# Value matmuls on 64x64 tiles of the array and energy matmuls on 64x128 tiles, one key chunk at a time

## The chip, the cores and the metric

The kernel runs on one core of a Trainium2 chip. The metric is the device time of one execution in microseconds (us), the median of several. A profile of one execution is kept for every kernel; all views below are of such profiles.

## The reference, cut to what matters

```python
# x: (4, 64, 96, 96) float32; layer 0 works on its group norm g
q = einsum('bchw,oc->bohw', g, wq) + bq      # 8 channels; k alike; v has 64
energy = einsum('bcn,bcm->bnm', Q, K)        # 9216 x 9216 for each of 4 batches
att = sigmoid(energy)
out = einsum('bcm,bnm->bcn', V, att) + g
# ... a channel gate on out, the residual, then layer 1: a spectral
# convolution (a truncated FFT as small matmuls). The change is in layer 0 alone.
```

The 4 batches are taken as 2 pairs. In a pair the 9216 queries are 18 blocks of 512 and the 9216 keys 72 chunks of 128. So there are 2 x 18 x 72 = 2592 chunk visits, and each needs energies of two batches, one sigmoid over 128 x 1024, and values of two batches.

## The kernel before

P = 128, NB = 512, C = 64, NCH = 72. Energies are made from high and low parts of q and k so that the one-pass type (fp32r) keeps fp32 accuracy: 8 channels x 4 combinations of parts are 32 rows. Two chunks and two batches lie on four groups of 32 rows.

```python
# PSUM: ps_s 3 buffers of 2 banks, ps_a 2 buffers of 1 bank
def energies(n, jj, q):                        # two chunks of keys at once
    es = [ps_s.tile([P, 2, NB], F32, tag="s", ...) for i in range(2)]
    for i in range(2):
        for b in range(2):
            r = slice(32 * (2 * i + b), 32 * (2 * i + b) + 32)
            nc.tensor.matmul(es[i][:, b, :], kT[r, jj, :], q[r, :], start=True, stop=True)
    # ... one sigmoid per chunk: at <- es[i] (ScalarE)

def values(acc, jj, ats):                      # plain fp32
    for i in range(2):
        j = 2 * jj + i
        for b in range(2):
            half = slice(b * C, (b + 1) * C)
            nc.tensor.matmul(acc[half, :], vT[:, j, half], ats[i][:, b, :],
                             start=(j == 0), stop=(j == NCH - 1))

for n in range(NBLK):
    acc = ps_a.tile([P, NB], F32, tag="a", ...)
    for jj in range(NCH // 2):
        nxt = energies(n, jj + 1, q)           # (of the next block at the end)
        values(acc, jj, ats); ats = nxt
        # ... q of the next block is projected eight steps before the end
    # ... VectorE adds acc to xn, sums and maxima for the gate
```

## Time and profile before

| | before |
|---|---|
| time, median of 3 | 3697.69 us (3696.52 to 3698.01) |
| matrix engine (PE) busy | 96% of the span |
| ScalarE busy | 70% |
| the attention loop, both pairs | about 3030 of 3695 us |

A timeline row gives the start and length in us, the engine, the source line, the operation with what it writes and reads, the tile of the array in rows*columns, the shape, and the number of instructions merged into the row. PEld is a weight load. Brackets hold the idle time of the engine before the row and what ended it; "issue" means that the profile shows nothing it waited for. The record of a matmul begins when it goes to the array (after a change of tiling that is when its own weight load begins, 1001.87 and 1001.88 in the view of the changed kernel), and its end is modelled, so the distances between starts are what to trust. Below, a pass is one matmul record, a round is the passes that start together on different tiles, and a visit is the rounds of one kind of matmul, energies or values, before the other kind follows. The prediction below shows the page and one step of the loop.

### The profile page before, as it was taken

To read this page: it belongs to the slowest core of one execution; us is meant where nothing else is said; L and a number is where in the kernel's file an instruction comes from. 1 tells how busy PE (TensorE), PEld (TensorE's weight loads), DVE (VectorE), ACT (ScalarE), POOL (GpSimd) and SP (SyncE) were. 2 spreads that over 40 slices of the span, in tenths; PEclk is the share of its full clock that TensorE was granted. 3 is DMA by queue.
4 is the path that set the end of the run, shared out by engine and by line. 5 is a ranking of instruction groups with operands and counts; after the bars stand their busy time and mean duration, and the time that the engine had idled before them with its cause. 6 is when DMAs were issued, how large, how long until landed. Compare 5 with 4: busy or idle time off the path is not lost.

```text
span 3694.8 us, 44562 instructions
## 1 busy us (share of the span) xinstructions
PE 3564.6 (96%) x19088; PEld 1391.2 (38%) x19088; DVE 424.2 (11%) x810; ACT 2585.2 (70%) x2699; POOL 2.9 (0%) x10
## 2 busy tenths in 40 slices
PE   5999999999999999969999999999999999699999
PEld 3222222222222222232222222222222222289999
DVE  7000000000000000061000000000000000431033
ACT  1888888888888888826888888888888888511011
POOL 0000000000000000000000000000000000000000
PEclk8999999999999999989999999999999999855555
DMA  2000000000000000000000000000000000000311
GB/s 107 1 1 1 1 1 1 1 1 1 1 1 1 1 1 1 1 0 1 1 1 1 1 1 1 1 1 1 1 1 1 1 1 1 35 1 23 126 49 55
DMA packets 7222, 38.93 MB, mean 11 GB/s; under 512 B 1936, under 2 KB 2416, under 8 KB 3952
## 3 DMA queue, kind: packets, MB, share of 16 engines
q1 hardware_dynamic: 5184, 35.65, 2.6%
q8 instruction: 149, 2.44, 0.3%
q10 hardware_dynamic: 1840, 0.43, 0.1%
q14 instruction: 49, 0.40, 0.0%
HBM read 26.65 MB, written 9.44 MB: 10 GB/s over the span
## 4 chain that ended last, share of the span: by engine, by line
PE 94%; DVE 4%; DMA 0%; issue 0%; ACT 0%; ACTq 0%; POOL 0%; POOLq 0%; DVEq 0%
PE acc L225 66%; PE e L211 15%; PE pv L335 3%; PE pa L304 2%; PE py L371 2%; PE pz L362 2%; PE pq L199 1%; DVE stats L113 1%; PE pu L316 1%; PE pu L319 1%; DVE x L270 1%; DVE vT L188 1%; DVE strip L135 0%; DVE low_k L144 0%; PE pvt L349 0%; PE proj L184 0%
## 5 line engine op out<-in xcount | busy, mean ns | idle before, releaser
L216 ACT ACTIVATE at<-e 128x1024 f32<-128x1024 f32 x2592 | 2512.6, 1021 | 657.7 <-PE e L211 657.7
L225 PE MATMUL acc<-at,vT 128*64 128x512 f32 x10368 | 2513.9, 606 | 0.0
L225 PEld LDWEIGHTS acc<-at,vT 128*64 128x64 f32 x10368 | 629.5, 136 | 1062.3 <-issue 1061.2
L211 PE MATMUL e<-q,kT 32*128 32x512 f32 x5184 | 660.1, 498 | 12.7 <-DVE q L148 11.3
L211 PEld LDWEIGHTS e<-q,kT 32*128 32x128 f32 x5184 | 248.8, 182 | 1062.3 <-issue 1059.4
L143 DVE TENSOR_SCALAR full_q<-pq,bq 128x512 f32<-128x512 f32 x36 | 27.0, 750 | 2266.0 <-PE pq L199 2266.0
L335 PE MATMUL pv<-u,wt 128*64 128x12 f32 x1024 | 109.4, 261 | 0.0
L335 PEld LDWEIGHTS pv<-u,wt 128*64 128x64 f32 x1024 | 109.3, 227 | 0.2 <-issue 0.2
L245 DVE SCALAR_TENSOR_TENSOR xn<-acc,xn 128x512 f32<-128x512 f32 x36 | 24.9, 692 | 622.8 <-PE acc L225 622.8
L304 PE MATMUL pa<-fw_sb,xT 96*96 96x48 f32 x512 | 84.4, 361 | 1.3 <-ACT xT L110 1.3
L304 PEld LDWEIGHTS pa<-fw_sb,xT 96*96 96x96 f32 x512 | 84.1, 257 | 1.8 <-ACT xT L110 1.8
L371 PE MATMUL py<-gw_sb,z 32*128 32x96 f32 x384 | 82.5, 417 | 1.8 <-ACT z L110 1.8
L371 PEld LDWEIGHTS py<-gw_sb,z 32*128 32x128 f32 x384 | 82.1, 328 | 2.5 <-ACT z L110 2.5
L362 PE MATMUL pz<-gh_sb,vt 64*32 64x96 f32 x512 | 82.3, 363 | 0.0
L362 PEld LDWEIGHTS pz<-gh_sb,vt 64*32 64x32 f32 x512 | 81.6, 171 | 0.3 <-issue 0.3
L110 ACT COPY v<-pv 64x192 f32<-64x192 f32 x16 | 7.6, 477 | 101.4 <-PE pv L335 101.4
L110 ACT COPY z<-pz 32x384 f32<-32x384 f32 x32 | 25.4, 795 | 57.2 <-PE pz L362 57.2
L110 ACT COPY a<-pa 96x384 f32<-96x384 f32 x16 | 12.8, 800 | 73.4 <-PE pa L304 73.4
L128 PE MATMUL pv_l<-t_l,pav 128*128 128x1 f32 x8 | 2.3, 359 | 49.3 <-DVE t_l L126 49.3
L110 ACT COPY xT<-pt 96x512 f32<-96x512 f32 x24 | 14.0, 582 | 50.9 <-PE pt L296 50.9
L184 PE MATMUL proj<-wv,xn 128*128 128x128 f32 x288 | 49.4, 323 | 0.0
L178 PE MATMUL proj<-xn,wk 128*64 128x256 f32 x144 | 28.4, 477 | 20.8 <-DVE xn L135 20.4
(65 smaller groups left out, 757.1 us busy)
## 6 DMA issues: line engine op xcount, KB each, us to landing
wt<-in_spec_dram SPq DMA_DIRECT2D x16, 1024.0 KB, 4.9
x<-in_x_dram SPq DMA_DIRECT2D x8, 1152.0 KB, 7.8
out_dram<-x SPq DMA_DIRECT2D x12, 768.0 KB, 3.2
fh_sb<-in_fh_dram ACTq DMA_DIRECT2D x1, 72.0 KB
pav<-in_pairavg_dram ACTq DMA_DIRECT2D x1, 64.0 KB, 5.7
wk<-in_wk_dram ACTq DMA_DIRECT2D x1, 64.0 KB
wq<-in_wq_dram ACTq DMA_DIRECT2D x1, 64.0 KB, 4.3
bv<-in_bv_dram ACTq DMA_DIRECT2D x2, 32.0 KB, 3.6
```

What stands on the lines that cost most here:

```text
L110: nc.scalar.copy(dst, src)
L113: nc.vector.bn_stats(stats[:, s, :], xt[:, bass.ts(s, NB)])
L184: nc.tensor.matmul(pp[:, 1, bass.ts(i, P)], xn[:, bass.ts(j, P)], wv_sb, start=True, stop=True)
L188: nc.vector.tensor_tensor(vT[:, 4 * s:4 * s + 4, :], pp[:, 1, :].rearrange("p (i m) -> p i m", m=P), bv_sb.rearrange("p b c -> p (b c)").u ...
L199: nc.tensor.matmul(pq, wq_sb, xn[:, bass.ts(n, NB)], start=True, stop=True)
L211: nc.tensor.matmul(es[i][:, b, :], kT[r, jj, :], q[r, :], start=True, stop=True)
L216: nc.scalar.activation(at, es[i], AF.Sigmoid)
L225: nc.tensor.matmul(acc[half, :], vT[:, j, half], ats[i][:, b, :], start=(j == 0), stop=(j == NCH - 1))
L304: nc.tensor.matmul(pa[:H, bass.ts(i, 3 * KW)], xT[:, :, 8 * g + i], fw_sb, start=True, stop=True)
L335: nc.tensor.matmul(pv[:C, bass.ts(kw, 3 * B)], wt[:, i, kw, :], u[:, kh, kw, :, :].rearrange("q s b -> q (s b)"), start=True, stop=True)
L362: nc.tensor.matmul(pz[:2 * KW, bass.ts(i, H)], vt[:, b, :, :, o].rearrange("q e k -> q (e k)"), gh_sb, start=True, stop=True)
L371: nc.tensor.matmul(py[:, bass.ts(i, W)], z[:, 4 * g + i, :], gw_sb, start=True, stop=True)
```

## The change

Its intent is to have energies and values on tiles with the same number of rows. Values sum the two 64-key halves of a chunk in two banks, on four 64x64 tiles. Energies take one chunk of both batches, 64 rows each (of which q's zeros switch off the 32 of the other chunk).

```diff
-            tc.tile_pool(name="ps_s", bufs=3, space=PSUM) as ps_s, \
+            tc.tile_pool(name="ps_s", bufs=2, space=PSUM) as ps_s, \
...
-            def energies(n, jj, q):
-                es = [ps_s.tile([P, 2, NB], F32, tag="s", name=f"e_{p}_{n}_{jj}_{i}")
-                      for i in range(2)]
-                for i in range(2):
-                    for b in range(2):
-                        r = slice(32 * (2 * i + b), 32 * (2 * i + b) + 32)
-                        nc.tensor.matmul(es[i][:, b, :], kT[r, jj, :], q[r, :], ...)
+            def energies(n, j):
+                e = ps_s.tile([P, 2, NB], F32, tag="s", name=f"e_{p}_{n}_{j}")
+                for b in range(2):
+                    r = slice(64 * b, 64 * b + 64)
+                    nc.tensor.matmul(e[:, b, :], kT[r, j // 2, :], qs[n][j % 2][r, :], ...)
...
-                        nc.tensor.matmul(acc[half, :], vT[:, j, half], ats[i][:, b, :],
+                    for r in range(2):
+                        keys = slice(64 * r, 64 * r + 64)
+                        nc.tensor.matmul(acc[half, r, :], vT[keys, j, half], at[keys, b, :],
...
-                acc = ps_a.tile([P, NB], F32, tag="a", name=f"acc_{p}_{n}")
-                for jj in range(NCH // 2):
+                acc = ps_a.tile([P, 2, NB], F32, tag="a", name=f"acc_{p}_{n}")
+                for j in range(NCH):
...                     # energies of chunk j + 2, then values of chunk j
-                nc.vector.scalar_tensor_tensor(blk, acc, 1.0, blk, ALU.mult, ALU.add,
+                nc.vector.scalar_tensor_tensor(blk, acc[:, 0, :], 1.0, blk, ALU.mult, ALU.add)
+                nc.vector.scalar_tensor_tensor(blk, acc[:, 1, :], 1.0, blk, ALU.mult, ALU.add,
                                                accum_out=sums[:, n:n + 1])
...                     # q in two versions (even, odd chunks), k on rows in another order,
                      # projected on four 32-column tiles instead of two of 64 columns
```

More of the change, by code (lines that the diff above doesn't have):

```diff
@@ L72, in tile_kernel @@
     bk_sb = const.tile([P, 1], F32, tag="bk", name="bk")
-    split_sb = const.tile([P, 4], F32, tag="split", name="split_sb")
+    split_sb = const.tile([P, 6], F32, tag="split", name="split_sb")
     nc.scalar.dma_start(wk_sb, wk4)
@@ L135, in normalize, with split_parts @@
         nc.vector.tensor_scalar(dst, src, mr[:, 0:1], mr[:, 1:2], ALU.subtract, ALU.mult)
-    def split_parts(dst, src, bias, which, pool, name):
+    def split_parts(dsts, src, bias, first, pool, name):
         n = src.shape[-1]
@@ L141, in split_parts @@
         high = pool.tile([P, n], F32, tag="high", name=f"high_{name}")
-        low = pool.tile([P, n], F32, tag="low", name=f"low_{name}")
         nc.vector.tensor_scalar(full, src, bias, None, ALU.add)
-        nc.vector.tensor_scalar(low, src, bias, split_sb[:, 2 * which + 1:2 * which + 2],
-                                ALU.add, ALU.mult)
         nc.vector.tensor_scalar(high.bitcast(U32), full.bitcast(U32), HIGH, None,
                                 ALU.bitwise_and)
-        nc.vector.scalar_tensor_tensor(dst, high, split_sb[:, 2 * which:2 * which + 1], low,
-                                       ALU.mult, ALU.add)
+        for i, dst in enumerate(dsts):
+            f = 2 * (first + i)
+            low = pool.tile([P, n], F32, tag=f"low{i}", name=f"low{i}_{name}")
+            nc.vector.tensor_scalar(low, full, split_sb[:, f + 1:f + 2], None, ALU.mult)
+            nc.vector.scalar_tensor_tensor(dst, high, split_sb[:, f:f + 1], low,
+                                           ALU.mult, ALU.add)
     stats1 = []
@@ L156, in tile_kernel @@
             tc.tile_pool(name="q", bufs=2) as qp, \
+            tc.tile_pool(name="parts", bufs=1) as partp, \
             tc.tile_pool(name="att", bufs=4) as attp, \
-            tc.tile_pool(name="ps_s", bufs=3, space=PSUM) as ps_s, \
+            tc.tile_pool(name="ps_s", bufs=2, space=PSUM) as ps_s, \
             tc.tile_pool(name="ps_a", bufs=2, space=PSUM) as ps_a:
@@ L175, in tile_kernel @@
                 pp = ps_s.tile([P, 2, NB], F32, tag="s", name=f"proj_{p}_{s}")
-                for e in range(2):
-                    rows = slice(64 * e, 64 * e + 64)
+                for r in range(4):
+                    rows = slice(32 * r, 32 * r + 32)
                     nc.tensor.matmul(
                         pp[rows, 0, :2 * P].rearrange("p (a m) -> p a m", m=P), wk_sb[:, rows],
-                        xn[:, cols].rearrange("p (a e m) -> p a e m", e=2, m=P)[:, :, e, :],
+                        xn[:, cols].rearrange("p (a e m) -> p a e m", e=2, m=P)[:, :, r % 2, :],
                         start=True, stop=True)
@@ L185, in tile_kernel @@
                                      start=True, stop=True)
-                split_parts(kT[:, 2 * s:2 * s + 2, :].rearrange("p a m -> p (a m)"),
-                            pp[:, 0, :2 * P], bk_sb, 0, qp, f"k_{p}_{s}")
+                split_parts([kT[:, 2 * s:2 * s + 2, :].rearrange("p a m -> p (a m)")],
+                            pp[:, 0, :2 * P], bk_sb, 0, partp, f"k_{p}_{s}")
                 nc.vector.tensor_tensor(
@@ L199, in project_q @@
                 nc.tensor.matmul(pq, wq_sb, xn[:, bass.ts(n, NB)], start=True, stop=True)
-                q = qp.tile([P, NB], F32R, tag="q", name=f"q_{p}_{n}")
-                split_parts(q, pq, bq_sb, 1, qp, f"q_{p}_{n}")
-                return q
-            def energies(n, jj, q):
-                es = [ps_s.tile([P, 2, NB], F32, tag="s", name=f"e_{p}_{n}_{jj}_{i}")
-                      for i in range(2)]
-                for i in range(2):
-                    for b in range(2):
-                        r = slice(32 * (2 * i + b), 32 * (2 * i + b) + 32)
-                        nc.tensor.matmul(es[i][:, b, :], kT[r, jj, :], q[r, :],
-                                         start=True, stop=True)
-                ats = []
-                for i in range(2):
-                    at = attp.tile([P, 2, NB], F32, tag="att", name=f"at_{p}_{n}_{jj}_{i}")
-                    nc.scalar.activation(at, es[i], AF.Sigmoid)
-                    ats.append(at)
-                return ats
@@ L220, in values @@
-            def values(acc, jj, ats):
-                for i in range(2):
-                    j = 2 * jj + i
-                    for b in range(2):
+                q = [qp.tile([P, NB], F32R, tag=f"q{e}", name=f"q{e}_{p}_{n}")
+                     for e in range(2)]
+                split_parts(q, pq, bq_sb, 1, partp, f"q_{p}_{n}")
+                return q
+            def energies(n, j):
+                e = ps_s.tile([P, 2, NB], F32, tag="s", name=f"e_{p}_{n}_{j}")
+                for b in range(2):
+                    r = slice(64 * b, 64 * b + 64)
+                    nc.tensor.matmul(e[:, b, :], kT[r, j // 2, :], qs[n][j % 2][r, :],
+                                     start=True, stop=True)
+                at = attp.tile([P, 2, NB], F32, tag="att", name=f"at_{p}_{n}_{j}")
+                nc.scalar.activation(at, e, AF.Sigmoid)
+                return at
@@ L224, in values @@
+            def values(acc, j, at):
+                for b in range(2):
+                    for r in range(2):
                         half = slice(b * C, (b + 1) * C)
-                        nc.tensor.matmul(acc[half, :], vT[:, j, half], ats[i][:, b, :],
+                        keys = slice(64 * r, 64 * r + 64)
+                        nc.tensor.matmul(acc[half, r, :], vT[keys, j, half], at[keys, b, :],
                                          start=(j == 0), stop=(j == NCH - 1))
-            q = project_q(0)
@@ L229, in tile_kernel @@
-            ats = energies(0, 0, q)
+            steps = [(n, j) for n in range(NBLK) for j in range(NCH)]
+            qs = {0: project_q(0)}
+            ahead = [energies(*steps[0]), energies(*steps[1])]
             for n in range(NBLK):
-                acc = ps_a.tile([P, NB], F32, tag="a", name=f"acc_{p}_{n}")
-                for jj in range(NCH // 2):
-                    nxt = None
-                    if jj + 1 < NCH // 2:
-                        nxt = energies(n, jj + 1, q)
-                    elif n + 1 < NBLK:
-                        nxt = energies(n + 1, 0, q)
-                    values(acc, jj, ats)
-                    ats = nxt
-                    if jj == NCH // 2 - 8 and n + 1 < NBLK:
-                        qn = project_q(n + 1)
-                    if jj == NCH // 2 - 2 and n + 1 < NBLK:
-                        q = qn
+                acc = ps_a.tile([P, 2, NB], F32, tag="a", name=f"acc_{p}_{n}")
+                for j in range(NCH):
+                    if n * NCH + j + 2 < len(steps):
+                        ahead.append(energies(*steps[n * NCH + j + 2]))
+                    values(acc, j, ahead.pop(0))
+                    if j == NCH - 16 and n + 1 < NBLK:
+                        qs[n + 1] = project_q(n + 1)
@@ L414, in four @@
         for r in range(4):
-            o[r % 2, :, r] = w.T[:, None]
+            o[r // 2, :, r] = w.T[:, None]
         return o.reshape(P, P)
-    high = np.stack([np.tile(np.repeat(h, C8), 4) for h in ([1, 1, 0, 0], [1, 0, 1, 0])], 1)
+    kh, qh = [np.tile(np.repeat(h, C8), 4) for h in ([1, 1, 0, 0], [1, 0, 1, 0])]
+    even = np.arange(P) // 32 % 2 == 0
+    parts = np.stack([2 * kh - 1, 1 - kh] + [m * f for m in (even, ~even)
+                                             for f in (2 * qh - 1, 1 - qh)], 1)
     sent = {
@@ L423 @@
         "wk4": four(l0["wk"]), "bk4": np.tile(l0["bk"], 16).reshape(P, 1),
-        "split": np.stack([2 * high - 1, 1 - high], 2).reshape(P, 4).astype(np.float32),
+        "split": parts.astype(np.float32),
         "wvT": l0["wv"].T, "bv": l0["bv"].reshape(1, C),
```

## The prediction

> **What bounds the kernel now.** I read the page first: busy shares, then the chain that ended last, then the costliest groups.
>
> ```profile
> PE 3564.6 (96%) x19088; PEld 1391.2 (38%) x19088; DVE 424.2 (11%) x810; ACT 2585.2 (70%) x2699; POOL 2.9 (0%) x10
> ...
> PE acc L225 66%; PE e L211 15%; PE pv L335 3%; PE pa L304 2%; PE py L371 2%; PE pz L362 2%; PE pq L199 1%; DVE stats L113 1%; PE pu L316 1%; PE pu L319 1%; DVE x L270 1%; DVE vT L188 1%; DVE strip L135 0%; DVE low_k L144 0%; PE pvt L349 0%; PE proj L184 0%
> ...
> L216 ACT ACTIVATE at<-e 128x1024 f32<-128x1024 f32 x2592 | 2512.6, 1021 | 657.7 <-PE e L211 657.7
> L225 PE MATMUL acc<-at,vT 128*64 128x512 f32 x10368 | 2513.9, 606 | 0.0
> ...
> L211 PE MATMUL e<-q,kT 32*128 32x512 f32 x5184 | 660.1, 498 | 12.7 <-DVE q L148 11.3
> ```
>
> The reader sees that value matmuls (L225) and energy matmuls (L211) are 81% of the chain, that they never wait long (0.0 and 12.7 us idle), and that ScalarE, which waits 657.7 us for energies, is not the bound. "128*64" and "32*128" are the array tiles: rows by columns. The counts also tell the passes: there are 2 pairs x 18 blocks x 36 = 1296 steps of two key chunks, each with four value and four energy matmuls. So 10368 value records are two passes per plain fp32 matmul, and 5184 energy records are one pass per fp32r matmul.
>
> A busy matrix engine is not one at its peak, so next I read the timeline of one step in the middle (start us, length us, engine, line, operation, count):
>
> ```profile
> 1001.80 0.19 PEld L211 LDWEIGHTS e<-q,kT 32*128 32x128 f32 x4 [0.81 <-issue]
> 1001.80 0.51 PE L211 MATMUL e<-q,kT 32*128 32x512 f32 x4
> 1002.23 0.20 PEld L225 LDWEIGHTS acc<-at,vT 128*64 128x64 f32 x4 [0.24 <-issue]
> 1002.24 1.94 PE L225 MATMUL acc<-at,vT 128*64 128x512 f32 x8
> 1002.40 1.94 ACT L216 ACTIVATE at<-e 128x1024 f32<-128x1024 f32 x2 [0.36 <-PE e L211]
> 1002.72 0.14 PEld L225 LDWEIGHTS acc<-at,vT 128*64 128x64 f32 x2 [0.29 <-issue]
> 1003.15 0.14 PEld L225 LDWEIGHTS acc<-at,vT 128*64 128x64 f32 x2 [0.29 <-issue]
> 1004.10 0.19 PEld L211 LDWEIGHTS e<-q,kT 32*128 32x128 f32 x4 [0.81 <-issue]
> ```
>
> One step is 1004.10 - 1001.80 = 2.30 us: 0.43 us from the energies' start to the values', 1.87 us from the values' start to the next energies'. Eight value passes on two column tiles are four rounds. The second round's start to the third's weights is 1003.15 - 1002.72 = 0.43 us; four rounds are 1.71 us. The values take 0.16 us more than that, and the four energy matmuls, all started together, take 0.43. The extra is the price of alternating.
>
> **What the Trainium skill says.** (1) "TensorEngine Tiling (Array Packing)", Key Properties: changing the tiling mode, not just the tile, drains the TensorE; its list of configurations has 64x128 and 64x64 as two different ones. (2) "TensorE: Matmul & The Clock Gate", LDWEIGHTS: a weight load takes columns / 1.2 ns whatever the rows: 53 ns for 64 columns, 107 for 128. The trace agrees with both: the first value round lasts 1002.72 - 1002.24 = 0.48, 0.05 over a later one (the weight load that nothing hides after a change), and the remaining 0.10 of the 0.16 is the drain ahead of the energies. The energies' 0.43 is then 0.107 of weights, about 0.22 of streaming, 0.10 of drain.
>
> The change rests on one question: does a change of columns alone, at the same number of rows, also drain? The trace of before has such changes. In the projections (timeline, clock 1.0):
>
> ```profile
> 34.93 0.65 PE L178 MATMUL proj<-xn,wk 128*64 128x256 f32 x4
> ...
> 35.51 1.16 PE L184 MATMUL proj<-wv,xn 128*128 128x128 f32 x8
> ...
> 36.51 1.02 PE L199 MATMUL pq<-xn,wq 128*128 128x512 f32 x2
> ...
> 37.46 0.65 PE L178 MATMUL proj<-xn,wk 128*64 128x256 f32 x4
> ```
>
> L178 is two rounds of 256 columns, 2 x 0.213 = 0.43, but L184 starts 0.58 later: 0.05 + 0.10 over. L184 to L199, both 128*128, is 1.00 for eight passes of 0.107: 0.86 plus one 0.107 of weights, no drain. L199 to L178 is 0.95 for two passes of 0.427: 0.10 over. All rows are 128 here; only the columns change. And in the last stage (timeline, clock about 0.5), with 64 rows on both sides:
>
> ```profile
> 3515.75 0.74 PE L349 MATMUL pvt<-ident,v 64*64 64x64 f32 x5
> 3516.42 0.85 PE L362 MATMUL pz<-gh_sb,vt 64*32 64x96 f32 x4
> ```
>
> Five matmuls in 0.74, the last 0.311 long, gives one each 0.107, so the last started at 3516.18, and L362 0.24 later: 0.13 more than the usual spacing (at half the clock). So a column change alone costs the drain.
>
> **The change part by part**, per two chunks.
>
> - Values: four matmuls per chunk of 64 rows x 64 columns, on all four quarters of the array, instead of two of 128 x 64. Twice the records (20736), but four at once: two rounds of 0.427 per chunk, as before. I take the four to run side by side because the trace shows two column tiles starting 7 ns apart and four row tiles starting within 0.01 us. (3) "PSUM - Partial Sum Buffer", the collision section, asks that different row tiles write different banks; the change does that (two banks of acc, hence two reads at the block's end). No run before shows 64x64 tiles four at once.
> - Energies: two matmuls of 64 rows, 64x128 tiles, per chunk instead of four 32-row ones per two chunks. Rows do not shorten a pass, so two visits of 0.43 instead of one: +0.43 us.
> - Changes of tiling: still values 64x64, energies 64x128, so columns still change, and now twice as often: four changes per two chunks instead of two. The energies' share is inside the 0.43 above; the values' second visit adds an unhidden load and a drain: +0.05 + 0.10 = +0.15.
> - Starting four tiles instead of two at 7 ns: two more starts in each visit, some +0.02.
>
> Per two chunks 2.30 + 0.43 + 0.15 + 0.02 = 2.90 us, so 1.45 per chunk. Times 1296: +0.60 x 1296 = +778 us, all on the chain, as PE has no slack here.
>
> - VectorE: splitting q now costs two low and two combining operations: 0.75 + 0.42 + 2 x about 0.5 + 2 x 0.75 = 3.7 us per block against 2.7; one more accumulator read per block, +0.69. A block lasts 84 us and VectorE is busy 70 of 1511 us there: hidden, but for about 1 us at the end of each pair. In the projections low_k is read from a full copy in SBUF and should fall from 535 ns to near 283 (what high_k takes): 36 x 0.25 = 9 us less, perhaps 6 on the path.
> - The energy buffer goes from three to two. Energies of chunk j+2 wait for the sigmoid of j. In the trace the sigmoid starts 0.60 after the energies and takes 1.02, done at 1.62; two chunks later is 2.90. No wait. ScalarE does the same 2592 sigmoids, 0.92 us apart at best (1.94 for two less 1.02), under 1.45: it idles more.
> - q's projection (36 insertions) stays as it is.
>
> Sum: 3697.7 + 778 - 6 + 1 = about 4471 us.
>
> **Rivals.**
>
> *The drain goes away* because both have 64 rows: then a chunk is 0.854 + 0.213, with little overhead 1.08 us, against 1.15 now: 2592 x 0.07 = 185 us less, about 3510. It is plainly the intent. For it: the widest change now is in rows. Against: the three column-only changes above, at 128 and at 64 rows, that cost 0.10 to 0.13 like the others.
>
> *Half of it goes away*: loads may be pulled ahead across a column-only change, or the drain of 64-row tiles be shorter. Saving 0.1 of each of four changes leaves 2.5 per two chunks: about 3950. Against: in L178 to L184 neither was saved.
>
> *The four value tiles do not run four at once* (two rows quarters taking turns at the array): two more rounds per chunk, +0.854 x 2592, some 6700. Against: the energies' four row tiles now write four banks at once without taking turns. Small.
>
> *ScalarE becomes the bound*: it needs 0.92 per chunk and would bind only below that; in no case.
>
> **Range and chances.** Within the main story the uncertain terms are the stagger (0 to 0.04 per two chunks, 0 to 50 us) and the drain from 64-row tiles (0.08 to 0.12, +-50 us). That gives 4400 to 4530. I give the main story 0.88, the vanished drain 0.07, the rest 0.05; a result within 2% would need just the wrong amount of saving.
>
> **What would show it right or wrong.** In the timeline of the changed kernel: energies to energies 1.45 us; energies' start to values' start still 0.43; first value round 0.48, then about 0.54 to the energies. ScalarE's wait for energies should about double (657.7 + 778 = about 1430). If the energies-to-values distance is 0.22, the drain rival is right; if value rounds are four per chunk, the third. Clocks should stay at 1.0 there.

## The result, and the profile after

The changed kernel took 4457.5 us (4457.0 to 4458.06, 4 runs) against 3697.85 us. The ratio is 1.2055, with a 95% interval of 1.2034 to 1.2076. A ratio is the mean time of one kernel's fast runs over that of the other's of the same rounds, so it is not quite the ratio of the medians.

From the page of the changed kernel, the busy shares, the chain that ended last, and the groups of the loop:

```profile
PE 4326.2 (97%) x29600; PEld 1529.7 (34%) x29600; DVE 469.4 (11%) x918; ACT 2727.3 (61%) x2699; POOL 2.9 (0%) x10
...
PE acc L225 59%; PE e L213 25%; PE pv L331 2%; PE pa L300 2%; PE py L367 2%; PE pz L358 2%; PE pq L202 1%; DVE stats L113 1%; PE pu L312 1%; PE pu L315 1%; DVE x L266 1%; DVE vT L190 0%; DVE strip L135 0%; PE pvt L345 0%; DVE kT L149 0%; DVE full_k L142 0%
...
L216 ACT ACTIVATE at<-e 128x1024 f32<-128x1024 f32 x2592 | 2654.7, 1024 | 1273.6 <-PE e L213 1270.5
L225 PE MATMUL acc<-at,vT 64*64 64x512 f32 x20736 | 2824.9, 615 | 0.0
L213 PE MATMUL e<-q,kT 64*128 64x512 f32 x5184 | 1298.2, 498 | 14.4 <-DVE q L149 13.4
```

The matrix engine still sets the end. The energies' records are as many as before (5184), but their share of the chain went from 15% to 25%: they stand in twice as many visits. ScalarE's wait for them doubled. One chunk of the changed kernel, from the timeline:

```profile
1000.43 0.50 PE L213 MATMUL e<-q,kT 64*128 64x512 f32 x2
1000.86 0.21 PEld L225 LDWEIGHTS acc<-at,vT 64*64 64x64 f32 x8 [0.24 <-issue]
1000.86 1.09 PE L225 MATMUL acc<-at,vT 64*64 64x512 f32 x8
1001.03 1.02 ACT L216 ACTIVATE at<-e 128x1024 f32<-128x1024 f32 x1 [0.42 <-PE e L213]
1001.87 0.19 PEld L213 LDWEIGHTS e<-q,kT 64*128 64x128 f32 x2 [0.81 <-issue]
1001.88 0.50 PE L213 MATMUL e<-q,kT 64*128 64x512 f32 x2
```

One chunk is 1001.88 - 1000.43 = 1.45 us: 0.43 from energies to values, 1.02 from values to energies. Before, 2.30 us did two chunks. The visit of the energies is as long as before (0.43) and does half the work. The clock in the loop is 1.0 in both kernels.

Where the 760 us are: averaged over all undisturbed steps, the distance between energies is 2.305 us per two chunks before and 1.4495 us per chunk after. So the loops give 1296 x (2.899 - 2.305) = +770 us. Ahead of the first energies the kernel is 3 us shorter (they start at 77.5 instead of 80.6), between the two pairs' loops 6 us shorter, and after the loops 2 us longer. From the first energies to the last values the two loops together grew by 768 us: 768 - 3 - 6 + 2 = 761, against 760 measured.

### The profile page after: what moved, and what is told of

Read it like the earlier page. It is cut to its first block, busy times and chain, and to the rows that moved or that the text cites. A ratio compares the mean times of both kernels' runs of the same rounds, so it can differ in the third digit from the quotient of the medians.

```text
span 4455.2 us, 65732 instructions
## 1 busy us (share of the span) xinstructions
PE 4326.2 (97%) x29600; PEld 1529.7 (34%) x29600; DVE 469.4 (11%) x918; ACT 2727.3 (61%) x2699; POOL 2.9 (0%) x10
## 3 DMA queue, kind: packets, MB, share of 16 engines
q1 hardware_dynamic: 5184, 35.65, 2.1%
## 4 chain that ended last, share of the span: by engine, by line
PE 95%; DVE 4%; DMA 0%; issue 0%; ACT 0%; ACTq 0%; POOL 0%; POOLq 0%; DVEq 0%
PE acc L225 59%; PE e L213 25%; PE pv L331 2%; PE pa L300 2%; PE py L367 2%; PE pz L358 2%; PE pq L202 1%; DVE stats L113 1%; PE pu L312 1%; PE pu L315 1%; DVE x L266 1%; DVE vT L190 0%; DVE strip L135 0%; PE pvt L345 0%; DVE kT L149 0%; DVE full_k L142 0%
## 5 line engine op out<-in xcount | busy, mean ns | idle before, releaser
L216 ACT ACTIVATE at<-e 128x1024 f32<-128x1024 f32 x2592 | 2654.7, 1024 | 1273.6 <-PE e L213 1270.5
L225 PE MATMUL acc<-at,vT 64*64 64x512 f32 x20736 | 2824.9, 615 | 0.0
L213 PE MATMUL e<-q,kT 64*128 64x512 f32 x5184 | 1298.2, 498 | 14.4 <-DVE q L149 13.4
L213 PEld LDWEIGHTS e<-q,kT 64*128 64x128 f32 x5184 | 483.2, 183 | 2115.6 <-issue 2107.6
L225 PEld LDWEIGHTS acc<-at,vT 64*64 64x64 f32 x20736 | 539.4, 131 | 634.9 <-issue 634.4
L149 DVE SCALAR_TENSOR_TENSOR q<-high_q,split_sb,low_q 128x512 fp32r<-128x512 f32 x72 | 50.7, 745 | 0.0
L113 DVE BATCH_NORM_STATS2 stats<-x 128x6 f32<-128x512 f32 x72 | 45.7, 679 | 11.3 <-DMA x<-in_x_dram 11.3
```

Of the source, the lines that this page charges most:

```text
L113: nc.vector.bn_stats(stats[:, s, :], xt[:, bass.ts(s, NB)])
L149: nc.vector.scalar_tensor_tensor(dst, high, split_sb[:, f:f + 1], low, ALU.mult, ALU.add)
L213: nc.tensor.matmul(e[:, b, :], kT[r, j // 2, :], qs[n][j % 2][r, :], start=True, stop=True)
L216: nc.scalar.activation(at, e, AF.Sigmoid)
L225: nc.tensor.matmul(acc[half, r, :], vT[keys, j, half], at[keys, b, :], start=(j == 0), stop=(j == NCH - 1))
```

## The experiments

The theory: the array pays at each change of tiling, whether rows or columns change. The pay is a drain of about 0.1 us and a weight load that nothing hides, and the change doubles the number of visits; the streaming of a second energy pass comes on top. "Drain" is the skill's word. The traces show the extra time, not what the array does in it. The rivals: (A) the loss comes from the 64-row tiles themselves, twice as many small matmuls that do not run side by side; (B) the energy buffers, two instead of three, make the matrix engine wait for the sigmoid; (C) equal rows did save something, and other costs hid it. Each run below gave a right result. Where only one run was made its state is unknown, but most differences are large, and the small ones (energies_alone, values_alone) are read from averages over the loop, where the clock is 1.0 in every run.

### No change of tiling at all: e64_f16

Energies go on four 64x64 tiles too, so that the loop stays in one tiling. The first build did this in fp32r, and the compiler refused it: the check of the instruction failed on the output's first partition, 64. (With the output at partition 0 alone the same matmuls compile.) So k and q are fp16 parts, with 11 bits in the high one.

```diff
-HIGH = 0xFFFFF000
+HIGH = 0xFFFFE000
-  kT ... F32R, q ... F32R
+  kT ... F16,  q ... F16
-  nc.tensor.matmul(e[:, b, :], kT[r, j // 2, :], qs[n][j % 2][r, :], start=True, stop=True)
+  for h in range(2):
+      k = slice(64 * h, 64 * h + 64)
+      nc.tensor.matmul(e[k, b, :], kT[r, j // 2, k], qs[n][j % 2][r, :], start=True, stop=True)
```

> Energies on 64x64 tiles like the values (four matmuls per chunk, both halves of the keys), so that the tiling never changes inside the loop. [...]the parts of k and q are fp16 (11 bits high, the rest low). Theory 1 (each change of tiling costs a drain of 0.10 us and a weight load that nothing hides, whatever changes, rows or columns): per chunk 0.854 for the values and 0.213 for the energies with little else, 1.07 to 1.10 us instead of 1.45, so about 3500 us, faster than both kernels. Rival A (the loss comes from 64-row tiles themselves: twice as many small matmuls that are issued or run one after another): no change, about 4450, or more, since there are more records per chunk. Rival B (the energy buffers, two instead of three, make the matrix engine wait for the sigmoid): no gain, with waits for ScalarE showing.

Measured: 3489.67 us against 3696.89 us for the kernel before in the same rounds; ratio 0.9438, interval 0.9423 to 0.9454. It beats both kernels. Its timeline:

```profile
1000.54 0.39 PE L215 MATMUL e<-q,kT 64*64 64x512 f16 x4
1000.55 0.36 PEld L227 LDWEIGHTS acc<-at,vT 64*64 64x64 f32 x8 [0.31 <-issue]
1000.76 1.03 PE L227 MATMUL acc<-at,vT 64*64 64x512 f32 x8
1001.19 0.12 PEld L215 LDWEIGHTS <-kT 64*64 64x64 f16 x4 [0.29 <-issue]
1001.62 0.39 PE L215 MATMUL e<-q,kT 64*64 64x512 f16 x4
```

Energies to values is now 0.22 us, and values to energies 0.86, exactly two rounds of 0.43. The weights of the values start with the energies (1000.55), and those of the next energies go at 1001.19, beside the second value round. Nothing drains, nothing waits for weights: one chunk is 1.07 us. ScalarE is now nearly full too, with a sigmoid of 1.02 us in every 1.07. Rival A falls, as this loop has more records per chunk than the changed kernel and is the fastest. Rival B falls too, as it has the same two energy buffers and no wait of note. In the changed kernel itself the waits of the energies' weights for the sigmoid are 8.0 us in all (`--waits`: total, times, longest):

```profile
PEld e L213 <- ACT at L216: 8.0, 6, 1.6
```

But the data type changed as well, hence the control.

### The control for fp16: e128_f16

```diff
-HIGH = 0xFFFFF000
+HIGH = 0xFFFFE000
-  kT ... F32R, q ... F32R
+  kT ... F16,  q ... F16
```

> Control for the run with 64x64 energies: fp16 parts in the changed kernel, energies still on 64x128 tiles. Theory 1: the tiling still changes twice per chunk, so 1.45 us per chunk and about 4450 us; at most 0.08 us per chunk less (about 4250) if fp16 weights load faster. If fp16 itself were what makes the other run fast, this one would be as fast, about 3500.

Measured: 4174.85 us (one run). Its timeline:

```profile
1001.11 0.10 PEld L213 LDWEIGHTS <-kT 64*128 64x128 f16 x2 [0.81 <-issue]
1001.12 0.39 PE L213 MATMUL e<-q,kT 64*128 64x512 f16 x2
1001.44 0.21 PEld L225 LDWEIGHTS acc<-at,vT 64*64 64x64 f32 x8 [0.23 <-issue]
1001.44 1.09 PE L225 MATMUL acc<-at,vT 64*64 64x512 f32 x8
1002.46 0.39 PE L213 MATMUL e<-q,kT 64*128 64x512 f16 x2
```

fp16 is worth 0.11 us per chunk (1.34 against 1.45), all of it in the energies' visit, 0.32 instead of 0.43. I had expected at most 0.08. The groups show what changed, first in this run, then in the changed kernel:

```profile
L213 PEld LDWEIGHTS <-kT 64*128 64x128 f16 x5184 | 248.3, 92 | 2115.9 <-issue 2101.2
```

```profile
L213 PEld LDWEIGHTS e<-q,kT 64*128 64x128 f32 x5184 | 483.2, 183 | 2115.6 <-issue 2107.6
```

A load is 92 ns instead of 183. The Trainium skill's page "TensorE: Matmul & The Clock Gate", section "Weight-path perf modes", says that a fast weight load comes on by itself for 128 weights that are not fp32. The trace agrees in direction. If nothing hides the load, that explains 91 of the 108 ns; the other 17 stay open. The 685 us between this run and e64_f16 are not the type, which is the same. They are the two changes of tiling per chunk: 2592 x (1.341 - 1.074) = 692 us, less a few where q's projection on the whole array changes the tiling in both (this last was not measured).

### The energies of the change alone: energies_alone

```diff
-  for r in range(2):
-      keys = slice(64 * r, 64 * r + 64)
-      nc.tensor.matmul(acc[half, r, :], vT[keys, j, half], at[keys, b, :], ...)
+  nc.tensor.matmul(acc[half, 0, :], vT[:, j, half], at[:, b, :], ...)
   # and one read of acc at the end of a block instead of two
```

> Only the energies of the change: one chunk of both batches at a time on 64x128 tiles, values as before on 128x64 tiles, one bank. Theory 1: per chunk 0.43 + 0.48 + 0.53 = 1.44 us, so about 4430 us: the same as the changed kernel less the starts of two more tiles. Equal rows or not makes no difference. Theory that equal rows help: this one is slower than the changed kernel, by the drains saved. Rival A: nearly back at 3700, as the values are large again.

Measured: 4415.93 us (one run).

```profile
1000.98 0.51 PE L213 MATMUL e<-q,kT 64*128 64x512 f32 x2
...
1001.41 1.08 PE L223 MATMUL acc<-at,vT 128*64 128x512 f32 x4
...
1002.42 0.50 PE L213 MATMUL e<-q,kT 64*128 64x512 f32 x2
```

1.44 us in this stretch, 0.43 and 1.01; 1.434 on average. Here rows change from 64 to 128 and columns from 128 to 64. In the changed kernel only columns change, and each step is the same length but for the starts of two more value tiles, 7 ns apart (2592 x 0.0155 = 40 of the 42 us between the two kernels). So equal rows saved nothing (rival C), and the energies alone bring nearly the whole loss.

No experiment changes rows alone, but the loops do so at each projection of q (the changed kernel):

```profile
164.38 1.12 PE L202 MATMUL pq<-xn,wq 128*128 128x512 f32 x2
165.44 0.50 PE L213 MATMUL e<-q,kT 64*128 64x512 f32 x2
```

From the second pass of the projection to the energies are 0.522 us, at 34 places in the kernel before (to 32x128) and 34 in the changed one, against 0.43 between passes. From the last value matmul to the energies are 0.522 us in the kernel before (rows and columns change) and 0.519 in the changed one (columns alone). All three kinds of change cost about 0.09 us.

### The values of the change alone: values_alone

```diff
-  nc.tensor.matmul(acc[half, :], vT[:, j, half], ats[i][:, b, :], ...)
+  for r in range(2):
+      keys = slice(64 * r, 64 * r + 64)
+      nc.tensor.matmul(acc[half, r, :], vT[keys, j, half], ats[i][keys, b, :], ...)
-  ps_a bufs=2, pq in ps_a
+  ps_a bufs=1, pq in ps_s      # eight banks in all; two reads of acc per block
```

> Only the values of the change: 64x64 tiles and two banks; energies as before, two chunks at once on four 32-row tiles. To fit, one accumulator instead of two, which costs a wait of about 1.2 us at each of 34 block ends (some 40 us). Theory 1: in the steady state 2.32 us per two chunks against 2.30 before, so about 3760 us in all. Rival A: the steady state is 2.9 us per two chunks, about 4450 us.

Measured: 3766.89 us (one run).

```profile
1000.74 0.51 PE L211 MATMUL e<-q,kT 32*128 32x512 f32 x4
...
1001.18 1.95 PE L227 MATMUL acc<-at,vT 64*64 64x512 f32 x16
...
1003.06 0.51 PE L211 MATMUL e<-q,kT 32*128 32x512 f32 x4
```

1003.06 - 1000.74 = 2.32 us per two chunks against 2.30 before. Sixteen passes on four tiles take what eight on two tiles took (1.88 against 1.87), so the four tiles do run side by side. Rival A falls once more. On average a step is 2.313 against 2.305 us, 10 us in all, of the 69 us. The rest is at the block ends: energies start at 857.60 and again at 859.27 with no values between, while VectorE reads the only accumulator (857.74 to 859.16). Such an extra stretch of 1.67 us stands at 34 block ends, 57 us, where I had expected 1.2 us at each. It belongs to the one accumulator of this experiment, not to the change.

### The same matmuls with half the changes: paired

```diff
-  for j in range(NCH):
-      ahead.append(energies(*steps[n * NCH + j + 2]))
-      values(acc, j, ahead.pop(0))
+  for j in range(0, NCH, 2):
+      for i in range(2): ahead.append(energies(*steps[n * NCH + j + i + 2]))
+      for i in range(2): values(acc, j + i, ahead.pop(0))
```

> The changed kernel with its work in another order only: energies of two chunks one after the other, then values of two chunks. Same matmuls, same tiles, half as many changes of tiling. Theory 1: per two chunks 0.64 for the energies (0.107 + 2 x 0.213 + 0.10) and 1.88 for the values, 2.52 us instead of 2.90, so about 3970 us; still 0.21 over the kernel before, which is the second energy pass. Theory that the loss is in the tiles and not in the changes: about 4450 us as the matmuls are the same. The sigmoid of the second chunk ends some 2.44 us after the visit's start, just ahead of its buffer's next use: a small wait for ScalarE may show.

Measured: 3997.09 us (one run).

```profile
1001.00 0.30 PEld L213 LDWEIGHTS e<-q,kT 64*128 64x128 f32 x4 [0.81 <-ACT at L216]
1001.00 0.73 PE L213 MATMUL e<-q,kT 64*128 64x512 f32 x4
...
1001.67 1.95 PE L225 MATMUL acc<-at,vT 64*64 64x512 f32 x16
...
1003.54 0.73 PE L213 MATMUL e<-q,kT 64*128 64x512 f32 x4
```

2.54 us per two chunks instead of 2.90, by order alone; 460 us of the 760 come back. The two energy rounds of a visit take 0.67 us, not twice 0.43. On average it is 0.663, 0.02 over my 0.64. Beside the weights stands a wait for ScalarE. It costs nothing visible: values to energies is 1.88 us on average, as in values_alone, where the energies' weights waited for ScalarE only 71 times (1260 here), so the sigmoid seems to have ended at about the time at which the drain ended anyway.

The other 300 us do not come from changes of tiling. Against the kernel before, a visit of the energies is 0.225 us longer on average (0.663 against 0.438): it holds two rounds where the 32-row tiles needed one for the same two chunks. 1296 x 0.225 = 292 us. So the loss has two parts: some 460 us for the doubled changes, some 300 us for the second energy pass.

### The streaming of one energy pass: e_twice

```diff
   for b in range(2):
-      nc.tensor.matmul(e[:, b, :], kT[r, j // 2, :], qs[n][j % 2][r, :], start=True, stop=True)
+      for _ in range(2):
+          nc.tensor.matmul(e[:, b, :], kT[r, j // 2, :], qs[n][j % 2][r, :], start=True, stop=True)
```

> The changed kernel with each energy matmul issued twice into the same place (the second overwrites the first with the same numbers; the result is right). A second pass in the same tiling should cost its streaming alone, 0.213 us: 1.66 us per chunk and about 5010 us. If the 0.43 us of an energy visit were streaming (two cycles per column) rather than load, streaming and drain, it would cost 0.43: 1.88 us per chunk and about 5570 us.

Measured: 5070.07 us (one run).

```profile
1001.68 0.74 PE L214 MATMUL e<-q,kT 64*128 64x512 f32 x4
...
1002.35 1.09 PE L226 MATMUL acc<-at,vT 64*64 64x512 f32 x8
...
1003.37 0.74 PE L214 MATMUL e<-q,kT 64*128 64x512 f32 x4
```

1.69 us per chunk instead of 1.45: the second pass cost 0.237 us on average, near the 0.213 expected and far from 0.43. So about 0.19 us of each 0.43 us visit is not streaming. My figure of 0.213 was 0.024 short, 60 us in the sum; where those 24 ns go I did not find out.

## Why the prediction was right, point by point

- **The bound.** Right: PE stays at 97% and the chain is its matmuls. No engine took over.
- **A change of columns alone costs the drain.** This was the step the forecast turned on, read from small corners of the trace of before. Shown: energies to values, and values to energies, are as long at equal rows (the changed kernel) as at unequal ones (energies_alone), and both fall to bare streaming when nothing changes (e64_f16). One of my readings was loose: L184 to L199 is not eight passes of 0.107 and one load of 0.107, which makes 0.96; the records are 0.21 apart once and 0.11 seven times, which makes the 1.00. That there is no drain in it stands.
- **Values: two rounds per chunk, four tiles at once.** Shown by values_alone, the one thing no earlier run had shown.
- **Energies: a second visit of 0.43 us.** Right in sum. Its inner split (0.107 load, 0.22 streaming, 0.10 drain) is about right: e_twice has 0.24 for a pass, where I had about 0.22, and e128_f16 takes 0.11 off with a faster load. The loads of 53 and 107 ns were estimates from the page's columns / 1.2 ns; in the trace of before, a first round is longer than a later one by 0.05 us for 64 columns (values) and 0.10 for 128 (L184).
- **0.15 for the values' second visit, 0.02 for the starts.** The sum was 2.90 us per two chunks and 2.90 was measured; the loops grew by 770 us where I had 778.
- **VectorE and the start.** The saving ahead of the two loops was 9 us, where I had 6. low_k went from 535 to 345 ns, not to 283, so this agreement is partly luck.
- **No wait on the buffers.** Right, with two buffers in the changed kernel and in the faster e64_f16 also.
- **ScalarE's wait.** I wrote about 1430 us; it is 1273.6. I took its busy time as fixed, but pairs of sigmoids had overlapped in the records before (1.94 us for two of 1.02) and single ones no longer do: its busy time rose from 2512.6 to 2654.7, by 142 us. In paired, where they come in pairs again, it is 2511.7. No effect on the time.

The rival in which the drain goes away had 3510 us. That is close to what e64_f16 gets, but by leaving columns unchanged as well as rows.

## What to carry to other kernels

When two kinds of matmul alternate on the array, count the changes of tiling and give each one its price from the trace: the start-to-start distance across it less the usual spacing. A tiling is rows and columns together: here making the rows equal saved nothing, while making both equal, or grouping the work so that it changes half as often, did. Before halving a group to fit a layout, ask how many more visits that makes, and how many more passes: the two were some 460 and 300 of the 760 us.

## What the Trainium skill lacked or had wrong

- "TensorEngine Tiling (Array Packing)", Key Properties: it says that a change of tiling mode drains, but gives no cost and does not say that columns alone, or rows alone, count. Here: about 0.09 us at full clock (0.52 from the last matmul before a change to the first after it, against 0.43 between passes) and 0.13 at half the clock (L349 to L362), plus the weight load that can no longer be hidden (0.05 us for 64 columns). In all 0.27 us per pair of changes, e128_f16 against e64_f16.
- The same page, Restrictions: it does not say that an fp32r matmul with its output at partition 64 is refused by the compiler. That put the 64x64 energies out of reach until fp16 parts were used (3489.67 us).
- "TensorE: Matmul & The Clock Gate", the measured packing table: its speedups hold inside one tiling and say nothing of alternating. Four 64x64 fp32 tiles ran as fast as two 128x64 ones here (1.88 against 1.87 us for two chunks). The page's back-to-back formula gives 0.216 us for 512 columns; that is what an fp16 round took in e64_f16 (0.216, energies to values), but a second fp32r pass in the same tiling cost 0.24, and the page has no figure for fp32r.
- "FP8 and Floating Point Precision", TensorE Precision Notes: it counts four passes for plain fp32. The time agrees (2 x 0.43 us for 512 columns in a stream, four times the 0.216 of fp16), but it does not say that a trace shows them as two records, which one needs to know to read counts such as 20736.
